# A four-layer graph network on one core: layer 0's work put in order by queues that know their buffers

## The chip, the cores and the metric

The kernel runs on one core of a Trainium2 chip. The core has five engines that each work through a queue of their own in order: TensorE (PE, matmuls), VectorE (DVE), ScalarE (ACT), GpSimd (POOL) and SyncE (SP, which here only starts transfers). They wait for one another through semaphores. The metric is the device time of one execution in microseconds (us), without the profiler. The kernel before takes 1137.64 us, the median of 3 runs (1135.74 to 1142.22). The profile is of one further execution under the hardware profiler, 1188.52 us long, with a span of 1186.5 us from the first to the last instruction.

## The reference, cut to what matters

Four graph layers on N = 4096 nodes with D = 64 features. `adj` is a dense 4096 x 4096 matrix of zeros and ones with about 4 ones in a row (probability 0.000976562).

```python
def _L0_gnn_ref(x, adj, r, w_att, b_att):            # hyperbolic attention
    c = 1.0 / r[0] ** 2
    x_t = logmap0(x, c)
    left, right = x_t @ w_att[:D, 0], x_t @ w_att[D:, 0]
    adj_att = sigmoid(left[:, None] + right[None, :] + b_att[0]) * adj
    x_local = logmap(x[:, None, :], x[None, :, :], c)
    support_t = jnp.einsum('ij,ijd->id', adj_att, x_local)
    return proj(expmap(x, support_t, c), c)
# layer 1: h_neigh = (adj @ X + X) / deg; relu([X, h_neigh] @ W + b), normalised by row
# layer 2: two hops of tanh([adj @ x, x] @ W[k])
# layer 3: weights 0.5 ** rank along each row of adj, w @ (x @ weight) + bias
h = relu(layernorm(x)); x = x + layer(h)             # around each of the four layers
```

Layer 0 needs a value for each pair of nodes that are joined. The kernel does not compute all 4096 x 4096 pairs: it finds the neighbours of each node in the matrix, gathers their rows, and computes only those.

## The kernel before: the parts that the change touches

The matrix is handled in 8 blocks `nb` of 512 columns (4 tiles of 128 nodes); two blocks make a group `g`. All layer 0 code below is written as Python generators: each `yield` is a point at which a loop at build time may switch to other work, and its number is the time which that loop assumes for the step. The order that comes out is fixed when the program is built; each engine then follows it.

Packing. A piece of a block (4 x 128 rows by 512 columns, 1 MB) is loaded, cast to fp8 for the later layers (blocks 0 to 2 stay on chip, the others are written to memory and read again after layer 0) and multiplied by powers of two on PE, so that 16 bits of the matrix become one number. `keys` holds the transposed numbers of a block in PSUM.

```python
        if part == 0:
            keys[b] = [psum.tile([P, 2, NW], F32, tag="k", bufs=2, name=f"keys{b}_{s}") for s in range(2)]
        pk = psum.tile([P, 512], F32, tag="pk", bufs=2, name=f"pk{u}")
        for v in range(4):
            at = part * 4 + v
            a = load(b, at)
            if b < EARLY:
                S.copy(a8[b][:, 4 * at : 4 * at + 4, :], a, saturate=False)
            else:
                f8 = strm.tile([P, 4, 512], FP8, tag="f8", name=f"f8_{b}_{at}")
                S.copy(f8, a, saturate=False)
                nc.scalar.dma_start(adj8[b][:, 4 * at : 4 * at + 4, :], f8.bitcast(BF16))
            bits = a.bitcast(BF16).rearrange("p j (i b) -> p j i b", b=2)
            for j in range(4):
                w = 4 * v + j
                T.matmul(
                    pk, wflat[:, w * P : (w + 1) * P], bits[:, j, :, 1], start=(w == 0), stop=(w == 15),
                )
            if v < 3:
                yield
        kt = l0w.tile([P, 512], F32, tag="kt", name=f"kt{u}")
        S.activation(kt, pk, AF.Identity, bias=num[:, part : part + 1])
        for k in range(LB):
            T.transpose(
                keys[b][k // 2][:, k % 2, part * P : part * P + P], kt[:, k * P : (k + 1) * P], sh.ident
            )
```

Lists. DVE finds for each node up to 4 neighbours (slots) and packs those that are over into a list for the block. Both parts then start gathers on GpSimd: 16 for the slots, 8 for the packed rows and their owners.

```python
    def lists(nb):
        ...
        for k in range(LB):
            kk = keys[nb][k // 2][:, k % 2, :]
            V.max(k16[:, k, :8], kk)
            V.match_replace(scr, k16[:, k, :8], kk, 0.0)
            V.max(k16[:, k, 8:], scr)
            yield 1.35
        turned[0] = nb + 1
        ...                      # neighbour numbers from the keys, into idx[nb]
        V.tensor_scalar_min(idx[nb], ji, N)
        yield 0.6
        gather_slots(nb)
        rem = tile_("rem", [LB, 48])
        cr = cand.rearrange("p k l w -> p k (l w)")
        V.tensor_tensor(rem, cr, j8[:, :, NS - 1 : NS].to_broadcast([P, LB, 48]), op=ALU.is_lt)
        V.tensor_mul(rem, rem, cr)
        ...                      # the rest into a packed list: ranks by a matmul (pb), sorted by a second (pc)
        V.tensor_scalar_min(own[nb], rw, float(N))
        yield 1.3
        gather_packed(nb)
        V.scalar_tensor_tensor(rw, ti, float(P), got[:, :, 1], op0=ALU.mult, op1=ALU.add)
        V.scalar_tensor_tensor(rw, rw, 1.0, ef, op0=ALU.add, op1=ALU.mult)
        yield 0.4
        ...
    def gather_slots(nb):
        g, q = divmod(nb, 2)
        if q == 0:
            es[g] = l0w.tile([P, 2, NE, TW], F32, tag="es", name=f"es{g}")
            hi[g] = l0w.tile([P, 2, NO, TW], F32, tag="hi", name=f"hi{g}")
        for k in range(LB):
            for s in range(NS):
                fetch(es[g][:, q, k * NS + s, :], idx[nb][:, k, s : s + 1])
```

Chunk, sums, finish. `chunk` takes the products of a gathered row with the node's own row. `sums` computes the weights, multiplies the rows by them (line 1053) and adds them up by matmuls into `v` (lines 1059 and 1065); with that the buffer `es` is free. The pool `l0w` has two buffers for each name, so `es` of group g + 2 takes the place of `es` of group g. `finish` (about 50 short operations on DVE) turns the sums of a group into its new rows of `x`.

```python
    def sums(g, q0, q1):

        part = slice(q0, q1)
        w = yield from weights(
            s_e[g][:, part, :], es[g][:, part, :, :], x2e[g][:, part, :], lfe[g][:, part, :], f"{g}_{q0}"
        )
        if q0 == 0:
            vs[g] = l0w.tile([P, 8, DQ], F32, tag="vs", name=f"vs{g}")
        for q in range(q0, q1):
            nb = 2 * g + q
            spot = l0w.tile([P, NO, 512], F32, tag="spot", name=f"spot{nb}")
            for c in range(NO):
                V.tensor_scalar(spot[:, c, :], io, rows_at[nb][:, c : c + 1], None, op0=ALU.is_equal)
                yield 0.4
            ek = es[g][:, q, :, :DQ]
            V.tensor_mul(ek, ek, bc(w[:, q - q0, :], DQ))
            yield 1.5
            bank = psum.tile([P, 512], F32, tag="v", bufs=2, name=f"v{nb}")
            pv = bank[:, : LB * DQ]
            slots = es[g][:, q, : LB * NS, :DQ].rearrange("p (k s) e -> p s k e", k=LB)
            for s in range(NS):
                T.matmul(
                    pv.rearrange("p (k e) -> p k e", k=LB), sh.ident, slots[:, s], start=(s == 0), stop=False,
                    skip_group_check=True,
                )
            for c in range(NO):
                for k in range(LB):
                    T.matmul(
                        pv[:, k * DQ : (k + 1) * DQ], spot[:, c, k * P : (k + 1) * P],
                        es[g][:, q, LB * NS + c, :DQ], start=False, stop=(c == NO - 1 and k == LB - 1),
                        skip_group_check=True,
                    )
            summed.add(nb)
            S.copy(vs[g][:, q * LB : q * LB + LB, :], pv.rearrange("p (k e) -> p k e", k=LB))
```

The order before. Lists come first whenever their keys are packed, then `chunk`, then `sums` and `finish` of a group as side work:

```python
        def can_pack():

            b, v = divmod(packed[0], 8)
            return b < NR and (v < 3 or turned[0] >= b)

        ...
        todo = [lists(nb) for nb in range(NR)]
        ...
        follow = {
            1: [sums(0, 0, 2), finish(0, 0, 8)],
            3: [sums(1, 0, 2), finish(1, 0, 8)],
            5: [sums(2, 0, 2), finish(2, 0, 8)],
            6: [sums(3, 0, 1)],
            7: [sums(3, 1, 2), finish(3, 0, 8)],
        }
        pending = []
        while listed < NR or pending or side:
            while can_pack() and arrived[packed[0]] <= now + 1.0:
                pack_one()
            job = None
            if listed < NR and packed[0] >= 8 * (listed + 1):
                job = todo[listed]
            elif pending and pending[0][1] <= now and (pending[0][0] < 4 or pending[0][0] // 2 * 2 - 3 in summed):
                job = pending[0][2]
            elif side:
                job = side[0]
        ...
```

Layer 1. `weigh` makes `y`, the weighed and normalised rows of a group in three bf16 parts, for each of four groups of 8 node tiles; `product` multiplies the matrix by it. At the first of its four steps it takes the chunks of the first three groups, then the `tail` that makes the last group, then that group's chunks:

```python
            if at == 0:
                for k in range(GR):
                    part(k, first)
                tail()
                for k in range(GR):
                    part(k, last)
                    end(k)
...
        for m in range(NQ - 1):
            weigh(m, ln_group(m, "ln1"), y3s[0], both(0), "l1", bias=b1_t)
...
        up, down = list(range(NQ)), list(reversed(range(NQ)))
        product(
            y3s[0], 3 * D + 1, "l1", up,
            lambda: weigh(NQ - 1, ln_group(NQ - 1, "ln1"), y3s[0], both(0), "l1", bias=b1_t),
            up, l1_done, lambda m: weigh(m, hs[m], y3s[1], both(1), "l2"), itself=True,
        )
```

## Time and profile before

| stretch of the span (us) | what runs | PE busy | DVE busy | POOL busy | moved, GB/s |
|---|---|---|---|---|---|
| 0 to 100 | rows of layer 0, packing, first lists | 42.15 | 58.26 | 33.51 | 268 |
| 100 to 200 | packing, lists, gathers | 42.23 | 57.72 | 65.82 | 289 |
| 200 to 300 | packing, lists | 51.68 | 67.85 | 3.46 | 277 |
| 332 to 392 | gathers of blocks 4 and 5 | 0.00 | 4.36 | 45.38 | 28 |
| 392 to 435 | sums | 13.33 | 26.07 | 0.07 | 2 |
| 435 to 495 | gathers of blocks 6 and 7 | 0.00 | 12.60 | 45.66 | 28 |
| 495 to 597 | sums and finishes | 27.24 | 59.99 | 0.00 | 1 |
| 597 to 638 | first weighings of layer 1 | 12.61 | 20.42 | 0.00 | 257 |

Over the whole span PE is busy for 699.4 us (59%), DVE for 550.2, ACT for 347.9 and POOL for 194.2. Layer 0 ends with the operation that writes `over` at 596.79 us.

How such lines are read: a row of digits is the span in 40 equal slices, and a digit is the busy share of a slice in tenths. A line of the waits names the engine and the source line that waited, after the arrow what it waited for, then the total in us, how many times, and the longest. A line of the timeline has the start and the length in us, engine, source line, operation, result and operands, and in brackets the idle time before it with what ended it. "Issue" stands for idle time which nothing in the profile explains, and "remote" for a semaphore whose writer the profile does not name.

### The profile page before, as it was taken

The page shows a single profiled execution, that of the slowest core. Times are in us where ns is not written, and L with a number is a line of the kernel's source. Part 1 is how long each engine was busy: PE and PEld are TensorE (multiplying, and loading weights), DVE is VectorE, ACT ScalarE, POOL GpSimd, SP SyncE. Part 2 cuts the span into 40 slices and gives each one's busy share as a digit, 9 for nine tenths or more (in the row PEclk, how much of TensorE's full clock was granted, in tenths as well). Part 3 has the DMA queues.
Part 4 walks back from the last instruction along what each step waited for, and adds up shares of the span by engine and source line. Part 5 has one row for each costly group of instructions (what it writes and reads, how often), then busy time and mean ns, then how long its engine had stood idle before and what let it go on. Part 6 is the DMA issues. An engine that isn't in the chain of part 4 may idle for free. (4 is left out here: it accounts for less than half of the span.)

```text
span 1186.5 us, 14354 instructions
## 1 busy us (share of the span) xinstructions
PE 699.4 (59%) x5602; PEld 527.3 (44%) x5602; DVE 550.2 (46%) x1705; ACT 347.9 (29%) x468; POOL 194.2 (16%) x208
## 2 busy tenths in 40 slices
PE   3453334456210040042226899899989779999997
PEld 1121111113110040032216899899989746565564
DVE  5746455776601622266554545422144434444443
ACT  4754344663000200113321111111112224343343
POOL 0375566000067127500000000000000000000000
PEclk9856556565565565565657999899999979999999
DMA  8788797996011001100080000000000000000000
GB/s 293 246 283 278 231 303 258 336 344 241 9 21 29 7 9 28 21 1 0 1 351 5 2 1 2 1 2 1 2 1 2 1 1 1 9 2 9 4 7 12
DMA packets 49248, 99.49 MB, mean 84 GB/s; under 512 B 6802, under 2 KB 6802, under 8 KB 48274
## 3 DMA queue, kind: packets, MB, share of 16 engines
q1 hardware_dynamic: 35232, 79.70, 19.0%
q0 software_dynamic: 6144, 6.80, 3.4%
q10 hardware_dynamic: 7794, 11.98, 2.7%
q8 instruction: 46, 0.75, 0.3%
q14 instruction: 32, 0.26, 0.1%
HBM read 85.79 MB, written 12.67 MB: 83 GB/s over the span
## 5 line engine op out<-in xcount | busy, mean ns | idle before, releaser
L1337 PEld LDWEIGHTS <-a 128*128 128x128 fp8e4 x3072 | 263.5, 98 | 12.6 <-issue 10.5
L785 PE MATMUL pk<-a,wpack 128*128 128x512 bf16 x256 | 110.4, 582 | 106.0 <-DMA a<-in_adj_t 79.5
L934 POOL DMA_INDIRECT es<-rows_d,idx x128 | 122.7, 959 | 248.5 <-PE v L1065 170.6
L1059 PE MATMUL v<-es,ident 128*128 128x260 f32 x64 | 26.3, 581 | 215.8 <-issue 208.1
L1479 DVE TENSOR_SCALAR wt<-cnt 128x512 int16<-128x512 f32 x128 | 88.5, 691 | 122.5 <-PE cnt L1472 122.5
L1480 ACT ACTIVATE wt<-cnt,low_t 128x512 int16<-128x512 f32 x128 | 87.9, 687 | 136.3 <-PE cnt L1472 136.3
L1059 PEld LDWEIGHTS v<-es,ident 128*128 128x128 f32 x64 | 17.9, 294 | 221.1 <-issue 208.5
L785 PEld LDWEIGHTS <-wpack 128*128 128x128 bf16 x256 | 32.4, 131 | 180.6 <-issue 166.5
L1459 PE MATMUL l_acc<-y_b,wt 128*128 128x192 bf16 x1024 | 107.7, 249 | 0.0
L1459 PEld LDWEIGHTS <-wt 128*128 128x128 bf16 x1024 | 90.0, 99 | 31.7 <-issue 2.4
L780 ACT CAST f<-a 128x2048 fp8e4<-128x2048 f32 x40 | 75.9, 1897 | 70.0 <-DMA a<-in_adj_t 46.4
L1337 PE MATMUL l_acc<-y_a,a 128*128 128x193 bf16 x1024 | 93.2, 250 | 3.6 <-DVE y_a L1307 3.6
L1483 PE MATMUL cnt<-a,fill 128*128 128x512 fp8e4 x248 | 81.7, 386 | 20.0 <-DVE wt L1479 20.0
L1337 PE MATMUL l2a_acc<-y_b,a 128*128 128x192 bf16 x1024 | 89.0, 249 | 2.9 <-DVE y_b L1307 2.9
L1337 PE MATMUL l2b_acc<-y_a,a 128*128 128x192 bf16 x1024 | 88.0, 247 | 3.0 <-DVE y_a L1307 3.0
L1472 PE MATMUL cnt<-a,tri 128*128 128x512 fp8e4 x256 | 77.8, 386 | 0.0
L777 ACT CAST a<-a 128x2048 fp8e4<-128x2048 f32 x24 | 45.2, 1893 | 20.7 <-DMA a<-in_adj_t 12.4
L965 DVE TENSOR_TENSOR pd<-es,tab 128x1024 f32<-128x1024 f32 x8 | 9.8, 1226 | 79.5 <-DMA es<-rows_d,idx 78.5
L1472 PEld LDWEIGHTS <-tri 128*128 128x128 bf16 x256 | 24.9, 98 | 37.3 <-issue 22.4
L793 PE MATMUL keys<-ident,kt 128*128 128x128 f32 x64 | 17.4, 425 | 39.6 <-ACT kt L791 22.7
L1483 PEld LDWEIGHTS <-fill 128*128 128x128 bf16 x248 | 24.2, 98 | 28.0 <-issue 21.3
L1065 PEld LDWEIGHTS v<-es,spot 128*128 128x128 f32 x256 | 34.6, 216 | 1.1
(336 smaller groups left out, 825.4 us busy)
## 6 DMA issues: line engine op xcount, KB each, us to landing
a<-in_adj_t SPq DMA_DIRECT2D x64, 1024.0 KB
adj<-f ACTq DMA_DIRECT2D x40, 256.0 KB
a<-adj SPq DMA_DIRECT2D x5, 2048.0 KB
es<-rows_d,idx POOLq DMA_INDIRECT x128
rows_d<-tab ACTq DMA_DIRECT2D x1, 1104.0 KB
x<-in_x SPq DMA_DIRECT2D x1, 1024.0 KB
out<-z SPq DMA_DIRECT2D x4, 256.0 KB
es<-rows_d,ovx POOLq DMA_INDIRECT x32
```

The costliest lines, as they stand in the source:

```text
L777: S.copy(a8[b][:, 4 * at : 4 * at + 4, :], a, saturate=False)
L780: S.copy(f8, a, saturate=False)
L785: T.matmul(pk, wflat[:, w * P : (w + 1) * P], bits[:, j, :, 1], start=(w == 0), stop=(w == 15),)
L934: G.indirect_dma_start(out=dst, out_offset=None, in_=rows_d, in_offset=bass.IndirectOffsetOnAxis(ap=at, axis=0))
L1059: T.matmul(pv.rearrange("p (k e) -> p k e", k=LB), sh.ident, slots[:, s], start=(s == 0), stop=False, skip_group_check=True,)
L1065: T.matmul(pv[:, k * DQ : (k + 1) * DQ], spot[:, c, k * P : (k + 1) * P], es[g][:, q, LB * NS + c, :DQ], start=False, stop=(c == NO - 1 an ...
L1337: T.matmul(acc, a8[n // 4][:, c, n % 4 * P : (n % 4 + 1) * P], y3[:, c, :cols], start=(c == first[0] and k % 2 == 0), stop=(c == last[-1] ...
L1459: T.matmul(accs[k // 2][:, k % 2, : 3 * D], wts[k // 4][:, (k % 4) * P : (k % 4 + 1) * P].bitcast(BF16), y3[:, c, : 3 * D], start=(c == NC ...
L1472: T.matmul(cnt[b], tri, masks[b], start=head_, stop=last, skip_group_check=True)
L1479: V.tensor_scalar(wts[0], cnt[0], -(128.0 - MAX_NEIGH) * UNIT, 0.0, op0=ALU.add, op1=ALU.max)
L1480: S.activation(wts[1], cnt[1], AF.Relu, bias=low_t)
L1483: T.matmul(cnt[b], fill, masks[b], start=False, stop=False, skip_group_check=True)
```

## The change

Layer 0's loop at build time is written anew. There are five queues of work: `list`, `chunk`, `sum`, `spot` and `finish`. Each piece of work knows what must be done before it, and a list stops (`HOLD`) ahead of its slot gathers until the `es` buffer that they write is free by the loop's clock. The loop counts the gathers that stand before GpSimd: with less than `BACKLOG` us of them it takes a list first, with more a chunk or a sum first. The comparison that finds a packed row's place (`spot`) is its own piece of work. The keys may take two blocks in PSUM, for which the banks of `s` and `v` fall from two to one each. In layer 1 the first product takes the chunks of `y` group by group: groups 0 and 1 are weighed, then come the matmuls of group 0, the weighing of group 2, the matmuls of group 1, the weighing of group 3, and the rest.

The diff, cut to its core (blank and unchanged lines are left out in places; "..." marks larger cuts):

```diff
@@ -47,6 +47,10 @@
 DQ = D + 1
 TW = D + 5
 NR = N // 512
+
+HOLD, FETCH = -1.0, 1000.0
+STREAM_AT, PACE_MB, PACKED = 7.0, 3.55, 5.0
+ROWS_AT, PACE_DMA, LANDED, SUMMED, BACKLOG, SLOW = 46.0, 1.27, 5.0, 6.0, 20.0, 1.1
@@ -768,7 +772,7 @@

-            keys[b] = [psum.tile([P, 2, NW], F32, tag="k", bufs=2, name=f"keys{b}_{s}") for s in range(2)]
+            keys[b] = [psum.tile([P, 2, NW], F32, tag="k", bufs=4, name=f"keys{b}_{s}") for s in range(2)]
@@ -853,7 +857,9 @@
         V.tensor_scalar(ji, ji, 2 * N - 1, None, op0=ALU.bitwise_and)
         V.tensor_scalar_min(idx[nb], ji, N)
         yield 0.6
+        yield HOLD
         gather_slots(nb)
+        yield FETCH + PACE_DMA * LB * NS
         rem = tile_("rem", [LB, 48])
         cr = cand.rearrange("p k l w -> p k (l w)")
         V.tensor_tensor(rem, cr, j8[:, :, NS - 1 : NS].to_broadcast([P, LB, 48]), op=ALU.is_lt)
...    (the one-bank change of "s" for pb and pc left out)
@@ -922,6 +928,7 @@
+        yield FETCH + PACE_DMA * 2 * NO
 ...
@@ -1033,7 +1040,14 @@
         yield 0.4
         return w
-    vs, summed = {}, set()
+    vs, spot = {}, {}
+
+    def spots(nb):
+
+        spot[nb] = l0w.tile([P, NO, 512], F32, tag="spot", name=f"spot{nb}")
+        for c in range(NO):
+            V.tensor_scalar(spot[nb][:, c, :], io, rows_at[nb][:, c : c + 1], None, op0=ALU.is_equal)
+            yield 0.48
     def sums(g, q0, q1):
@@ -1042,17 +1056,13 @@
-            vs[g] = l0w.tile([P, 8, DQ], F32, tag="vs", name=f"vs{g}")
+            vs[g] = l0w.tile([P, 8, DQ], F32, tag="vs", bufs=4, name=f"vs{g}")
-            spot = l0w.tile([P, NO, 512], F32, tag="spot", name=f"spot{nb}")
-            for c in range(NO):
-                V.tensor_scalar(spot[:, c, :], io, rows_at[nb][:, c : c + 1], None, op0=ALU.is_equal)
-                yield 0.4
-            bank = psum.tile([P, 512], F32, tag="v", bufs=2, name=f"v{nb}")
+            bank = psum.tile([P, 512], F32, tag="v", bufs=1, name=f"v{nb}")
@@ -1063,11 +1073,10 @@
-                        pv[:, k * DQ : (k + 1) * DQ], spot[:, c, k * P : (k + 1) * P],
+                        pv[:, k * DQ : (k + 1) * DQ], spot[nb][:, c, k * P : (k + 1) * P],
-            summed.add(nb)

@@ -1181,57 +1189,95 @@
             next(units[packed[0] // 4])
             packed[0] += 1
+        def arrives(m):
+            return STREAM_AT + PACE_MB * (m + 1)
         def can_pack():
             b, v = divmod(packed[0], 8)
-            return b < NR and (v < 3 or turned[0] >= b)
+            return b < NR and (v < 3 or turned[0] >= b - 1)
         row_stage(pack_one)
-...    (the loop before, whose core is shown above)
+        row_rest()
+        clock = {"now": ROWS_AT, "pool": ROWS_AT + 6.0}
+        landed, freed, done = {}, {}, set()
+        def list_ready(nb):
+            return arrives(8 * nb + 7) + PACKED if packed[0] >= 8 * nb + 8 else None
+        def list_hold(nb):
+            g = nb // 2
+            return freed.get(g - 2) if g > 1 else 0.0
+        def list_done(nb):
+            landed[nb] = clock["pool"] + LANDED
+        def sums_done(nb):
+            if nb % 2:
+                freed[nb // 2] = clock["now"] + SUMMED
+        def after(*names):
+            return lambda nb: clock["now"] if all(n in done for n in names) else None
+        class Job:
+            def __init__(self, kind, nb, gen, ready, end=None):
+                self.kind, self.nb, self.gen, self.ready, self.end = kind, nb, gen, ready, end
+                self.held = False
+        def freed_by(nb):
+            return [("sum", nb // 2 * 2 - 1)] if nb > 1 else []
+        queues = {k: [] for k in ("list", "chunk", "sum", "spot", "finish")}
+        for nb in range(NR):
+            g, q = divmod(nb, 2)
+            queues["list"].append(Job("list", nb, lists(nb), list_ready, list_done))
+            queues["chunk"].append(Job("chunk", nb, chunk(nb), landed.get))
+            queues["spot"].append(Job("spot", nb, spots(nb), after(("list", nb), *freed_by(nb))))
+            if g == NQ - 1:
+                queues["sum"].append(
+                    Job("sum", nb, sums(g, q, q + 1), after(("chunk", nb), ("spot", nb)), sums_done)
+                )
+            elif q:
+                need = [(k, n) for k in ("chunk", "spot") for n in (nb - 1, nb)]
+                queues["sum"].append(Job("sum", nb, sums(g, 0, 2), after(*need), sums_done))
+            if q:
+                queues["finish"].append(Job("finish", nb, finish(g, 0, 8), after(("sum", nb))))
+        while any(queues.values()):
+            now = clock["now"]
+            while can_pack() and arrives(packed[0]) <= now + 1.0:
                 pack_one()
+            hungry = clock["pool"] - now < BACKLOG
+            order = ["list", "chunk", "sum", "spot", "finish"] if hungry else ["chunk", "sum", "list", "spot", "finish"]
+            heads = [queues[k][0] for k in order if queues[k]]
+            times = []
+            for job in heads:
+                at = list_hold(job.nb) if job.held else job.ready(job.nb)
+                if at is not None:
+                    times.append((max(at, now), job))
+            runs = [job for at, job in times if at <= now]
+            if not runs:
+                waits = [at for at, _ in times]
                 if can_pack():
+                    waits.append(arrives(packed[0]))
+                clock["now"] = max(now + 0.1, min(waits))
                 continue
+            job = runs[0]
+            job.held = False
             try:
+                step = next(job.gen)
+                if step == HOLD:
+                    job.held = True
+                elif step >= FETCH:
+                    clock["pool"] = max(clock["pool"], now) + step - FETCH
+                else:
+                    clock["now"] = now + SLOW * step
             except StopIteration:
+                queues[job.kind].pop(0)
+                done.add((job.kind, job.nb))
+                if job.end is not None:
+                    job.end(job.nb)
         V.tensor_reduce(over, flags.rearrange("p b f -> p (b f)"), AX.X, ALU.add)
@@ -1318,7 +1364,8 @@
-    def product(y3, cols, name, made, tail, order, done, beside, itself=False):
+    def product(y3, cols, name, made, tail, order, done, beside, itself=False, behind={}):
@@ -1351,8 +1398,11 @@
                     done(m, k // 2, accs[k // 2], agg)

             if at == 0:
-                for k in range(GR):
-                    part(k, first)
+                for g in made[:-1]:
+                    for k in range(GR):
+                        part(k, range(g * GR, g * GR + GR))
+                    if g in behind:
+                        behind[g]()
                 tail()
                 for k in range(GR):
                     part(k, last)
@@ -1383,9 +1433,13 @@
         hs = {}
         V.memset(y3s[0][:, :, 3 * D : 3 * D + 1], 1.0)
-        for m in range(NQ - 1):
+        dgs = {}
+
+        def first_y(m):
             weigh(m, ln_group(m, "ln1"), y3s[0], both(0), "l1", bias=b1_t)
-        dgs = {}
+
+        first_y(0)
+        first_y(1)
         def l1_done(m, k2, acc, agg):
             if k2 == 0:
@@ -1413,9 +1467,9 @@

-            y3s[0], 3 * D + 1, "l1", up,
-            lambda: weigh(NQ - 1, ln_group(NQ - 1, "ln1"), y3s[0], both(0), "l1", bias=b1_t),
+            y3s[0], 3 * D + 1, "l1", up, lambda: None,
+            behind={0: lambda: first_y(2), 1: lambda: first_y(3)},
```

## The prediction

> **What bounds the kernel now.** I read the page's busy slices first, then the waits, then the timeline of single engines where the slices were empty. The slices (40 of them, 29.7 us each):
>
> ```profile
> PE   3453334456210040042226899899989779999997
> DVE  5746455776601622266554545422144434444443
> POOL 0375566000067127500000000000000000000000
> DMA  8788797996011001100080000000000000000000
> ```
>
> The DMA row says that the adjacency streams in until slice 9, about 300 us. From 300 to 597 us nothing streams and no engine is full; PE is busy only from slice 21 on. Those 297 us are the tail of layer 0. GpSimd (POOL) gathers neighbour rows in slices 1 to 6, not at all in 7 to 10, and again in 11 to 16. The waits of the DVE and POOL queues say why:
>
> ```profile
> POOL es L934 <- PE v L1065: 170.6, 2, 127.4
> DVE pd L965 <- DMA es<-rows_d,idx: 78.5, 3, 32.2
> ```
>
> The gathers into `es` wait for the matmuls that read the `es` of two groups before (two buffers, a group is two blocks of 512 columns): 170.6 us in two waits. The POOL timeline has both:
>
> ```profile
> 331.74 0.94 POOL L934 DMA_INDIRECT es<-rows_d,idx  x1 [127.37 <-PE v L1065]
> ...
> 434.93 0.94 POOL L934 DMA_INDIRECT es<-rows_d,idx  x1 [43.23 <-PE v L1065]
> ```
>
> And DVE, in the same stretch, starves first for keys and then for the gathers it delayed:
>
> ```profile
> 302.02 0.43 DVE L815 MAX8 k<-keys 128x8 f32<-128x256 f32 x1 [13.10 <-PE keys L793]
> ...
> 322.93 1.50 DVE L1053 TENSOR_TENSOR es<-es,w 128x1300 f32<-128x1300 f32 x1
> 353.23 1.23 DVE L965 TENSOR_TENSOR pd<-es,tab 128x1024 f32<-128x1024 f32 x1 [28.79 <-DMA es<-rows_d,idx]
> ```
>
> The product with `w` at 322.93 is the sum of block 1, though the lists of blocks 4 to 7 stand before it on DVE; only after it and its matmuls (324.49 to 331.47) may POOL gather block 4. So layer 0 runs: all lists, then two blocks of gathers (60 us), two sums, two more blocks (60 us), the rest. It is an order problem; no engine is the bound. From 597 us on the kernel is different: the chain that ended last is PE matmuls, 589 us that this change hardly touches.
>
> **Profiled and plain time.** The profiled execution took 1188.52 us, the median of the times is 1137.64: 51 us less. Layers 1 to 3 run at PE's pace, so I put the 51 us into layer 0. There DVE often waits over 1 us on nothing but its own last operation:
>
> ```profile
> 493.33 0.17 DVE L1139 TENSOR_TENSOR f_f<-f_f,f_den 128x8 f32<-128x8 f32 x1 [1.23 <-DVE f_a L1138]
> 496.13 0.17 DVE L1142 TENSOR_TENSOR f_y<-f_f,f_hs 128x8 f32<-128x8 f32 x1 [2.63 <-remote]
> ```
>
> Summed from the waits of DVE whose releaser is "DVE", "issue" or "remote": 10.8 (78 to 96 us), 14.6 (117 to 136), 8.9 (160 to 174), 5.6 (174 to 210), 21.8 (476 to 503), together 61.7, all while gathers run. I choose to read them as a cost of profiling. Layer 0 then ends at 597 - 51 = 546 us in a plain run.
>
> **What the Trainium skill says.** "Perfetto Trace Analysis", § Optimization Strategy: look at the gaps of the engine that should be full and at the semaphore that ends them; a repeated bubble can mean that there is no room for the next tile. The trace agrees: 127.4 and 43.2 us, both ended by the last reader of an `es` buffer. The same page, § DMA Instruction — SWDGE (GPSIMD): a gather's slice ends with its descriptors, not with the data. The trace agrees: the last gather of block 4 ends at 361.52, DVE reads its rows at 364.05, 2.5 us later. "SBUF — State Buffer", § SBUF: two separate sides: some DVE operations lock GpSimd out while it writes descriptors. Here it is small: the gathers average 959 ns against an undisturbed 940. "TensorE: Matmul & The Clock Gate", § What's actually happening: the array runs at half clock until it has been busy for about 3.4 us. In layer 1, 17 matmuls took 2.93 us (172 ns each) at 635 us, then 175 took 15.05 (86 ns).
>
> **The change part by part.** No operation is added or removed in layer 0; instruction counts per engine stay. What moves:
>
> 1. Lists stop before their gathers (HOLD) until the `es` buffer is free; the sums of group 0 now stand on DVE after the first half of list 3, those of group 1 before the second half of list 6. That takes away both POOL waits.
> 2. Keys get two blocks of PSUM (4 tiles for 2), so the stream no longer stops for the list of the block before; `s` and `v` fall to one bank each.
> 3. All of `finish` goes to the end but the first pieces of group 0.
> 4. Layer 1: the matmuls of y groups 0 and 1 are issued ahead of weighing groups 2 and 3.
>
> Pieces, from undisturbed stretches: a list 302.02 to 323.02, 21.0 us (11.2 to its slots); chunk 3.2; weights 412.27 to 418.14, 5.9; spots 1.6 and product 1.5 a block; finish 396.06 to 412.27, 16.2; v matmuls of two blocks 421.33 to 434.66, 13.3, of one 7.0; gathers 331.74 to 361.82, 30.1 a block (20.0 slots, 10.1 packed).
>
> Floors of the new layer 0. DVE: 50 us of rows (first list at 49.72), 8 x (21.0 + 3.2 + 1.6 + 1.5) = 218, 5 x 5.9 = 30, 4 x 16.2 = 65: 363 us. POOL: first gather 61.2, plus 8 x 30.1 = 302, plus landing, chunk, weights, product, sum and one finish, about 34: 336. Stream: 7 casts from 263.27 to 283.07 make 3.3 us a transfer, 64 of them 211 us, some 235 with disturbances. So DVE becomes the bound of layer 0.
>
> DVE does not run without gaps. Walking the new order with these pieces: list 0 done at 74 (its last part waits for block 1's packing); lists 1 and 2 at 96 and 121; list 3's slots at 141; sums of group 0 out of PE at 162, and list 3's count matmul stands behind them on PE, so DVE waits some 10 us; list 4's slots at 182, when `es` has been free since 162 and POOL has just finished block 3 (181); lists 4 and 5 at 194 and 219; list 6's slots at 234; spots, weights and products of group 1 to 246, matmuls to 260. POOL gathers block 6 from 260 to 280, its packed rows to 290, block 7 to 310 and 320. DVE: second half of list 6 to 267, list 7's first half 278, weights and product of group 2 to 285, list 7 done 296, chunk 6 at 299. The activations of block 6's weights stand on ACT behind the copy of block 5's sum (308): 5 us; weights 6 done 315, chunk 7 at 329, weights 7 and product 336. The next tanh stands behind the copy of the last sum (343), another 8 us; finish 0 done 354, then three more of 16: 402 us.
>
> Sum: layer 0 from 546 to 402, -144 us.
>
> Layer 1 before:
>
> ```profile
> 634.98 2.93 PE L1337 MATMUL l_acc<-y_a,a 128*128 128x193 bf16 x17
> 638.42 15.05 PE L1337 MATMUL l_acc<-y_a,a 128*128 128x193 bf16 x175 [0.51 <-DVE y_a L1307]
> ```
>
> PE does nothing but weighing from 597 to 635 and finishes the first eight column tiles at 666.5. A weighing takes 13.3 us; four of them end at 652. With 128 of the 256 matmuls done between weighings, 128 x 86 ns = 11 us remain after the third, of which the last 64 (6 us with the identities) after the fourth: about 659. Gain 7.5; the cold clock may eat some, I take -6.
>
> 1137.6 - 144 - 6 = 988 us.
>
> **Rivals.** (a) The DVE waits of over 1 us are real and not the profile's. Then the new order, which keeps POOL busy beside DVE almost throughout, meets them in every block: at 10 us a block, 80 us more on an engine that is now the bound; 1050 to 1070. For it: they appear only beside gathers. Against: the 51 us between profile and times need an owner. (b) The stream becomes the bound: sums put before packing on PE (13.3 us a pair) and ACT copies that wait for them hold back casts, with three stream buffers of 3.5 us each. One pair costs about 5 us, and DVE has that slack: 988 to 1000. (c) The schedule's assumed durations are off, and heads of the in-order queues block one another (PE waits for a list, DVE for PE): each 10 us more; 1000 to 1030. (d) DVE and ACT overlap better than my walk: down to the DVE floor, 363 instead of 402: 950. (e) Gathers still gate the end: POOL's 336 lies below 402, so no.
>
> **Range and chances.** (b) and (c) are more likely than (d), and (a) has perhaps one chance in seven; so 988 with 958 to 1035. Even (a) is faster by over 2% (under 1115). Slower needs a block that no part of the trace shows. Faster 0.96, same 0.02, slower 0.02.
>
> **What would show it.** Right: POOL's waits for `v` fall from 170.6 us to under 40; the DMA row ends near slice 8 or 9 of a shorter span; DVE at seven tenths or more from 50 us to the end of layer 0; `over` near 402 us plus what profiling adds; first product of layer 1 finished some 62 us after `over`, not 69.7. Wrong: POOL again waiting long for PE, DVE gaps named PE or ACT of over 10 us in a row, gaps on its own results in the plain time too, or a later stream.

## The result, and the profile after

The kernel after took 1023.8 us (median of 4 runs, 1019.2 to 1025.6), the kernel before 1136.7 us beside it (4 runs): a ratio of 0.900, 95% interval 0.895 to 0.904. Predicted were 988 us with 958 to 1035 as the range. So the direction and the mechanism held, and 36 us of the predicted gain of 150 did not come.

The busy slices of the kernel after (25.6 us each):

```profile
PE   3545556555622630017999989998996899999996
DVE  4769775769278548864455531113444345444443
POOL 0347777676067500000000000000000000000000
DMA  8699997999011100072000000000000000000000
```

The hole in the POOL row, four slices wide before, is one slice here (slice 10). DMA streams until slice 9, and PE's full stretch, layers 1 to 3, begins at slice 18. DVE has the seven tenths or more that I expected in only 9 of the 15 slices from 50 us to the end of layer 0 (2 to 16): it falls to 2 in slice 10 and to 5 and 4 in slices 13 and 14.

What POOL and DVE waited for, from the table of waits. The first line is from the waits of the whole span, the others from those of DVE between 259 and 440 us, the tail behind the last keys (line, what released it, us in total, times, longest):

```profile
POOL es L941 <- PE v L1075: 34.9, 1, 34.9
...
DVE spot L1049 <- PE v L1075: 15.9, 2, 9.2
DVE e L1018 <- ACT y L1016: 14.7, 4, 6.4
DVE f_f L1129 <- ACT f_f L1127: 10.4, 4, 9.5
DVE f_u L1096 <- ACT f_s L1114: 5.6, 1, 5.6
```

POOL's wait for `v`, 170.6 us in the profile the prediction read, is down to 34.9. What DVE waits for in the tail is neither keys nor gathers: it is the matmuls of the sums (the first of these lines) and short activations on ACT (the other three), 46.6 us in all.

The last keys and `over`, the end of layer 0, from the timelines of PE and of DVE:

```profile
259.69 1.11 PE L797 MATMUL keys<-ident,kt 128*128 128x128 f32 x4 [1.21 <-ACT kt L795]
```

```profile
439.98 0.18 DVE L1281 TENSOR_REDUCE over<-flags 128x1 f32<-128x32 f32 x1
```

From `over` to the end are 583.6 us.

### The profile page after: what moved, and what is told of

Same layout as the page of the kernel before. It is cut to its first block, busy times and chain, and to the rows that moved or that the text cites. A ratio compares the mean times of both kernels' runs of the same rounds, so it can differ in the third digit from the quotient of the medians.

```text
span 1023.6 us, 14344 instructions
## 1 busy us (share of the span) xinstructions
PE 705.4 (69%) x5602; PEld 532.8 (52%) x5602; DVE 551.8 (54%) x1705; ACT 344.2 (34%) x465; POOL 200.5 (20%) x208
## 3 DMA queue, kind: packets, MB, share of 16 engines
q1 hardware_dynamic: 35232, 79.70, 21.5%
## 4 chain that ended last, share of the span: by engine, by line
PE 49%; DVE 5%; ACT 3%; issue 1%; ACTq 0%
PE l2b_acc L1384 9%; PE l2a_acc L1384 9%; PE l_acc L1513 8%; PE l_acc L1384 8%; PE cnt L1537 7%; PE cnt L1526 5%; PE l_u L1344 1%; PE l_t L1331 1%; ACT l_h L1333 1%; DVE l_agg L1365 1%; PE l2b_u L1344 0%; PE l_u L1338 0%; DVE l_r L1351 0%; DVE ln_c L1609 0%; DVE ln_c L1615 0%
## 5 line engine op out<-in xcount | busy, mean ns | idle before, releaser
L941 POOL DMA_INDIRECT es<-rows_d,idx x128 | 128.1, 1001 | 95.3 <-issue 35.0
L1075 PEld LDWEIGHTS v<-es,spot 128*128 128x128 f32 x256 | 38.8, 238 | 1.2
L1075 PE MATMUL v<-es,spot 128*128 128x65 f32 x256 | 37.8, 318 | 0.0
L1365 DVE TENSOR_REDUCE l2a_agg<-l2a_acc 128x128 f32<-128x384 f32 x16 | 8.9, 558 | 51.4 <-PE l2a_acc L1384 51.4
```

The costliest lines, as they stand in the source:

```text
L941: G.indirect_dma_start(out=dst, out_offset=None, in_=rows_d, in_offset=bass.IndirectOffsetOnAxis(ap=at, axis=0))
L1075: T.matmul(pv[:, k * DQ : (k + 1) * DQ], spot[nb][:, c, k * P : (k + 1) * P], es[g][:, q, LB * NS + c, :DQ], start=False, stop=(c == NO - ...
```

## Experiments

Twelve runs in three groups. The groups did not meet the same chip. On chip A (first and third group) the kernel before took 1139.3 and 1138.1 us; on chip B (second group) 1182.7. Only kernels on chip A are compared with one another by their us.

**The kernel before, profiled again** (chip A; no edit).

> The kernel before, profiled a second time. My reading in the prediction: the DVE waits on its own results (61.7 us in the first profile) are a cost of profiling this kernel, so they return: a span of about 1186 us, layer 0 to its end near 597 us, plain time near 1137. Rival: that one profile was disturbed by chance; then this profile's span is within 10 us of the plain 1137 us, layer 0 ends near 547 us, and the DVE self-waits are gone, as they are in the profile of the kernel after.

Measured: a span of 1131.4 us, layer 0 ending at 541.5. The profiled execution itself took 1133.5 us, no longer than the 23 others on this chip (1134.2 to 1147.9). The waits of DVE on itself are gone: those that the trace puts down to "DVE", "issue" or "remote" make 0.6 us between 50 and 480 us; by the same count they were 53 in the first profile. The busy slices of this profile (28.3 us each), POOL's wait for the sums, and from PE's timeline the last keys of layer 0 (start, length, what it waited for):

```profile
PE   3355555461100400422268998999899689999997
DVE  5768777767015316565544554221244434444443
POOL 0367773000672177000000000000000000000000
DMA  8799999960110011000800000000000000000000
```

```profile
POOL es L934 <- PE v L1065: 149.1, 2, 105.7
```

```profile
255.86 1.12 PE L793 MATMUL keys<-ident,kt 128*128 128x128 f32 x4 [2.46 <-ACT kt L791]
```

The rival held, in this form: the first profile belongs to other conditions than the times beside it. It is not a cost of profiling. The second group points to the conditions. On chip B the kernel before takes 1182.7 us, near the first profile's 1188.5, and the kernels profiled there show the self-waits again: 61 to 98 us between 50 and 480 us, with two long waits at the spots (12.1 and 17.5 us) left out, since at the spots DVE waits for matmuls on chip A. Here is the largest group of them in one of these kernels, the version with the sums' matmuls behind the count (below):

```profile
DVE k L822 <- remote: 11.4, 6, 2.3
```

They are in the time, but on one of the two chips only. Two things follow. Taking 51 us off layer 0 led to the right start (546 against 541.5), by a wrong reason. And the second profile shows something that the first hid: on chip A the last keys of the kernel before are there at 256 us, not at 301. So 45 of the 55 us by which layer 0 is longer in the first profile lie ahead of the last keys, where the stream is. DVE is not alone in waiting there: SP, which starts the transfers, waits 58.4 us on "remote" within the first 320 us of the first profile and 4.6 in the second.

**Layer 1 alone** (chip A). The kernel before with the last two parts of the diff, layer 1's, and nothing else:

```diff
+                for g in made[:-1]:
+                    for k in range(GR):
+                        part(k, range(g * GR, g * GR + GR))
+                    if g in behind:
+                        behind[g]()
...
+            behind={0: lambda: first_y(2), 1: lambda: first_y(3)},
```

> Kernel before with the change of layer 1 alone (sums of the first y groups issued ahead of later weighings). Theory: 6 us of the gain, so about 1131 us plain, ratio 0.995; from the end of layer 0 to the end of the program 583.6 us as in the kernel after, against 589.7 before. Rival: it gains nothing by itself, because the matmuls run at half clock after the weighings' pauses: 1137, ratio 1.000, and the rest stays at 589 us.

Measured: 1135.7 us, ratio 0.996 (0.994 to 0.999). From the end of layer 0 to the end of the program: 1133.5 - 548.9 = 584.6 us, in the kernel before 1131.4 - 541.5 = 589.9. PE ahead of the fourth weighing and behind it:

```profile
586.75 7.39 PE L1337 MATMUL l_acc<-y_a,a 128*128 128x193 bf16 x64
...
599.61 6.83 PE L1337 MATMUL l_acc<-y_a,a 128*128 128x193 bf16 x72
```

64 matmuls (7.39 us) now run between the third weighing and the fourth; they are 115 ns each instead of the 86 at which PE ran 175 of them before. The gain is 5.3 us by the traces, 3.6 by the times, whose interval holds both. The theory held.

**Copies of the sums late** (chip A). In the kernel after, ACT's copy of `v` out of PSUM is issued right behind the matmuls of the sum. Here it is issued only when the bank is needed again or a `finish` begins:

```diff
+    def copies():
+        while late:
+            late.pop()()
 ...
+            copies()
             bank = psum.tile([P, 512], F32, tag="v", bufs=1, name=f"v{nb}")
 ...
-            S.copy(vs[g][:, q * LB : q * LB + LB, :], pv.rearrange("p (k e) -> p k e", k=LB))
+            late.append(
+                lambda to=vs[g][:, q * LB : q * LB + LB, :], pv=pv: S.copy(to, pv.rearrange("p (k e) -> p k e", k=LB))
+            )
 ...     (at the head of finish)
+        copies()
```

> Kernel after, with the ACT copy of each group sum out of PSUM issued only just before the bank is needed again or a finish reads it. Theory: of the 38 us that layer 0 is longer than predicted, 21 us are DVE waiting for ACT instructions that stand behind such a copy (5.9 at 345 us, 5.6 at 361, 9.5 at 383). Then layer 0 ends near 419 us and the time is about 1003 us, ratio to before 0.882. Rival: DVE only meets the matmuls of the last block a little later and waits there for the same end; then it gains under 6 us, 1018 or more.

Measured: 997.2 us, ratio to before 0.874 (0.868 to 0.880); the kernel after on the same chip (below) 1021.2. So 24 us come from moving eight instructions of 0.38 us each. How that comes about is seen best in the kernel after, in ACT's timeline, each line with its start, its length and in brackets what it waited for:

```profile
341.24 0.38 ACT L1080 COPY vs<-v 128x260 f32<-128x260 f32 x1 [6.60 <-PE v L1075]
341.63 1.28 ACT L1009 ACT_TABLE_LOAD   x1
342.93 0.22 ACT L1009 ACTIVATE w<-w 128x20 f32<-128x20 f32 x1
...
359.65 0.38 ACT L1080 COPY vs<-v 128x260 f32<-128x260 f32 x1 [13.00 <-PE v L1075]
359.93 0.63 ACT L1114 ACTIVATE f_s<-f_sup 128x512 f32<-128x512 f32 x1
...
381.54 0.38 ACT L1080 COPY vs<-v 128x260 f32<-128x260 f32 x1 [10.54 <-PE v L1075]
381.94 1.28 ACT L1127 ACT_TABLE_LOAD   x1
383.23 0.21 ACT L1127 ACTIVATE f_f<-f_a 128x8 f32<-128x8 f32 x1
```

ACT stands still for 6.6, 13.0 and 10.5 us, its queue's head waiting for PE, and the activations behind the copy (`w` and `y`, `f_s`, `f_f`) belong to other work, whose data are there. DVE in the same kernel waits for just these:

```profile
344.71 0.18 DVE L1018 TENSOR_TENSOR e<-y 128x20 f32<-128x20 f32 x1 [5.94 <-ACT y L1016]
360.59 0.69 DVE L1096 TENSOR_REDUCE f_u<-f_s 128x8 f32<-128x512 f32 x1 [5.58 <-ACT f_s L1114]
383.47 0.23 DVE L1129 SCALAR_TENSOR_TENSOR f_f<-f_f,rc_i,un_y 128x8 f32<-128x8 f32 x1 [9.53 <-ACT f_f L1127]
```

That is 21.0 us in sum. With late copies the same three instructions of DVE (the third line of code is L1137 there):

```profile
333.37 0.18 DVE L1018 TENSOR_TENSOR e<-y 128x20 f32<-128x20 f32 x1 [1.20 <-ACT y L1016]
...
343.55 0.68 DVE L1104 TENSOR_REDUCE f_u<-f_s 128x8 f32<-128x512 f32 x1
...
356.79 0.23 DVE L1137 SCALAR_TENSOR_TENSOR f_f<-f_f,rc_i,un_y 128x8 f32<-128x8 f32 x1 [0.28 <-ACT f_f L1135]
```

Two of the waits are nearly gone, and the first keeps 1.2 us, the activations themselves. DVE is busy for as long behind the last keys as in the kernel after (122.4 us against 122.5), but from the last keys to `over` it takes 413.3 - 258.9 = 154 us instead of 440.0 - 259.7 = 180. The theory held, but the 21 us are those of one profile. In the second profile of the kernel after (below) the same three waits are 5.9, 2.2 and 8.3 us, 16.4 in sum, and its tail is 16.2 us longer than with late copies. With 1.5 us left of them, 15 to 20 of the 24 us are traced to these waits. DVE's waits at the spots are 10.1 us here, 15.9 in the first profile of the kernel after and 11.0 in the second, so that difference is not shown to come from the copies.

**Spots later** (chip A). The two spots of a block are scheduled 12 us behind the sum that frees their buffers:

```diff
+        def spot_ready(nb):
+            if ("list", nb) not in done:
+                return None
+            if nb < 2:
+                return clock["now"]
+            at = freed.get(nb // 2 - 1)
+            return None if at is None else at + SPOT_LATE
 ...
-            queues["spot"].append(Job("spot", nb, spots(nb), after(("list", nb), *freed_by(nb))))
+            queues["spot"].append(Job("spot", nb, spots(nb), spot_ready))
```

> Kernel after, with the spots of a block scheduled only 12 us later than the end of the sum whose buffers they take, so that other work stands on DVE meanwhile. Theory: the two waits of DVE for matmuls at the spots of blocks 4 and 5 (9.2 and 6.7 us) are a loss on the path, DVE fills them with finish 0 and half lists, and they disappear: 16 us off, about 1008 us, ratio 0.887. Rival: DVE reaches the next wait earlier and the 16 us come back there (gathers of blocks 6 and 7 set the end): 1020 to 1026, ratio 0.90.

Measured: 1029.7 us, ratio 0.901 (0.896 to 0.907); `over` at 452.3. The waits at the spots are gone from DVE's list, the head of which is now:

```profile
DVE at L891 <- PE pb L882: 32.8, 5, 17.5
DVE f_u L1096 <- ACT f_s L1114: 18.5, 2, 10.3
...
DVE un_e L675 <- ACT un_y L673: 15.8, 4, 14.6
```

`finish 0` moved ahead, as wanted, and its activations now stood behind copies of sums: 8.3 us at 290, where ACT's copy of `v` waited for PE, and 14.6 us at 356, behind two such copies; a later `finish` 10.3 at 409. The theory failed. The waits came back, as the rival said, but not where it said, at the gathers of blocks 6 and 7 (DVE waits under 1 us for gathers here), and the time is above its range, 6 to 8 us over that of the kernel after: a gap that other work is meant to fill is worth nothing while that work needs the engine that is held up. The last keys also came 8 us later (267.8), which is not traced further.

**Less to write during the stream, kernel after** (chip B), and **with late copies** (chip A). Only the first of five fp8 blocks is written back, and layers 1 to 3 read that one for all five, so that their values are not those of the whole adjacency; 8.4 MB less are moved during the stream.

```diff
-                nc.scalar.dma_start(adj8[b][:, 4 * at : 4 * at + 4, :], f8.bitcast(BF16))
+                if b == EARLY:
+                    nc.scalar.dma_start(adj8[b][:, 4 * at : 4 * at + 4, :], f8.bitcast(BF16))
 ...
-        nc.sync.dma_start(a8[b].bitcast(BF16), adj8[b])
+        nc.sync.dma_start(a8[b].bitcast(BF16), adj8[EARLY])
```

> Kernel after, in which only the first of the five adjacency blocks that are written back as fp8 is written (layers 1 to 3 read that one block five times, so their values are not those of the reference); 8.4 MB of some 84 MB that the DMA engines move during the stream fall away. Theory: the stream is bound by the DMA engines (their share stands at 1.02 to 1.05 in most of it) and its last block is packed at 257 us instead of the 237 that I walked; with a tenth less to move it ends near 235 us, and as the tail hangs on the last keys, layer 0 ends 10 to 20 us earlier, 420 to 430 instead of 440; time 1004 to 1014. Rival: the stream waits for casts and packs (PE and ACT order), not for bytes; then its end moves by under 6 us and the time stays at 1018 to 1026.

> The late copies of sums together with four of five fp8 blocks not written back (layers 1 to 3 read one block five times, so their values are not the reference's). On a chip where the kernel with late copies takes 997 us: theory, the stream is bound by the bytes that the DMA engines move (share 1.04), 8.4 MB of 84 less end it 15 to 24 us before 259.6 and layer 0 ends 10 to 20 us before 413: time 977 to 988. Rival: the stream waits for casts, packs and lists; its end moves by under 6 us, time 990 to 999. On a chip of the slower kind the stream is uneven (slices of 142 to 340 GB/s) and I expect under 10 us of either.

On chip B: 1089.8 us, ratio 0.921 (0.917 to 0.926), last keys at 303 us. There is no run of the kernel after on that chip, so this one tells nothing of the stream; both theories stay open by it. On chip A: 984.0 us against 997.2 with late copies alone, ratio to before 0.864 (0.859 to 0.869), `over` at 398.3 instead of 413.3. The last keys of the kernel with late copies, and then of this one:

```profile
258.88 1.12 PE L797 MATMUL keys<-ident,kt 128*128 128x128 f32 x4 [1.21 <-ACT kt L795]
```

```profile
243.26 1.11 PE L798 MATMUL keys<-ident,kt 128*128 128x128 f32 x4 [0.78 <-ACT kt L796]
```

A tenth less to move brings the last keys 15.6 us earlier and the end of layer 0 by 15.0; the times differ by 13.2. The tail behind the last keys is as long as before (154 and 155 us). The theory held on chip A: what the DMA engines have to move bounds the stream. The edit also takes 32 DMA issues of 0.33 to 0.40 us from ACT's queue, but ACT is not what the stream waits for: between 50 and 260 us its casts wait 72.7 us for pieces to arrive with late copies alone, and still 63.3 us with less written. A rival stays open: SP starts a transfer only when one of the three stream buffers is free (with late copies alone it waits 163.9 us for the packing matmuls that read them), and no run varied their number.

**Keys of one block, kernel after** (chip B), and **with late copies** (chip A).

```diff
-            keys[b] = [psum.tile([P, 2, NW], F32, tag="k", bufs=4, name=f"keys{b}_{s}") for s in range(2)]
+            keys[b] = [psum.tile([P, 2, NW], F32, tag="k", bufs=2, name=f"keys{b}_{s}") for s in range(2)]
 ...
-            return b < NR and (v < 3 or turned[0] >= b - 1)
+            return b < NR and (v < 3 or turned[0] >= b)
```

> Kernel after with keys of one block again (two tiles, and packing of a block's fourth quarter transfer waits until the lists of the block before have read theirs). Theory: the second block's keys are what lets the stream run without stops, so without them the stream ends 15 to 30 us later and the time is 1040 to 1055, ratio 0.92. Rival: with sums and lists in the new order the lists follow the keys at once, and one block of keys does as well: 1020 to 1030, ratio 0.90.

> The late copies of sums, with keys of one block only. Where late copies alone take 997 us: theory, keys of two blocks are what lets the stream run on while DVE is busy with sums, so without them the stream ends 15 to 30 us later than 259.6 and the time is 1010 to 1025. Rival: lists follow their keys at once in the new order and one block does as well: 995 to 1002.

On chip B: 1094.3 us, ratio 0.926 (0.923 to 0.929); again with nothing there to compare it to. On chip A: 996.6 us, ratio 0.873 (0.868 to 0.878), against 997.2 and 0.874 with two blocks. Its last keys:

```profile
257.42 1.11 PE L797 MATMUL keys<-ident,kt 128*128 128x128 f32 x4 [1.21 <-ACT kt L795]
```

No difference in the time. With one block PE waits 5.8 us for DVE to have read the keys, and with two it never does, but the last keys come no earlier for it. The rival held: this part of the change gains nothing in the new order with late copies, on chip A.

**The assumed pace of the stream** and **the sums' matmuls behind the count** (both chip B, both with late copies), then **both together** (chip A).

```diff
-STREAM_AT, PACE_MB, PACKED = 7.0, 3.55, 5.0
+STREAM_AT, PACE_MB, PACKED = 7.0, 3.9, 5.0
```

```diff
         for q in range(q0, q1):
-            nb = 2 * g + q
             ek = es[g][:, q, :, :DQ]
             V.tensor_mul(ek, ek, bc(w[:, q - q0, :], DQ))
             yield 1.5
+        yield BEHIND
+        for q in range(q0, q1):
+            nb = 2 * g + q
             copies()
             bank = psum.tile([P, 512], F32, tag="v", bufs=1, name=f"v{nb}")
```

At `BEHIND` the loop first takes the list that stands between its slots and its count matmul on to that matmul.

> Kernel after with the late copies of sums (which took it to 997 us) and the schedule's assumed time of a transfer set to 3.9 us instead of 3.55, which is what the trace shows (64 transfers in some 250 us). The schedule then puts the weights of group 1 ahead of list 6 and its sums inside the stream. Theory: DVE has some 36 us of gaps between 100 and 250 us that such work can fill, and in the tail it is never idle for long, so what moves ahead of the last keys comes off the end: 10 to 15 us, 983 to 988, layer 0 ends near 400. Rival: the sums' matmuls on PE hold up packing and the stream ends later by as much: 993 to 1002.

> Kernel after with the late copies of sums, and the matmuls of a sum issued behind the count matmul of the list that stands beside it on DVE. The waits of DVE for that count (22.7 us in all, 9.6 at 172 us, 5.3 at 229) mostly disappear. Theory: they lie in the stretch that the stream bounds, so they cost nothing: within 5 us of 997, at most the last of them counts. Rival (what the prediction walked): DVE is the bound and each of them comes off the end: 977 to 983.

> Late copies of sums, the assumed 3.9 us a transfer, and the sums' matmuls behind the list's count matmul, together: the version that should be best. Theory, on a chip where late copies take 997: some 17 us of DVE work move ahead of the last keys, and the waits for the count (22.7 us) go; layer 0 ends at 390 to 400 instead of 413, time 974 to 986. Rival: packing is held up by as much, 992 to 1000. On a chip of the slower kind: 1060 to 1072, as its two parts alone (1075 and 1071).

On chip B: 1074.6 us (ratio 0.909, 0.904 to 0.913) and 1070.6 us (0.906, 0.902 to 0.910). Late copies alone were not run there, so neither of the two is judged. On chip A, both together: 994.2 us, ratio 0.871 (0.866 to 0.876), beside 997.2 and 0.874 (0.868 to 0.880): the intervals overlap, the two are not told apart. The last keys and DVE's waits of the version with both:

```profile
273.82 0.66 PE L797 MATMUL keys<-ident,kt 128*128 128x128 f32 x4 [0.78 <-ACT kt L795]
```

```profile
DVE spot L1056 <- PE v L1085: 21.5, 4, 8.0
...
DVE at L894 <- PE pb L884: 2.7, 4, 1.1
```

The waits for the count did go, from 22.7 to 2.7 us, and the tail fell from 154 to 409.2 - 273.8 = 135 us; but the last keys came 15 us later, and the waits at the spots doubled (10.1 to 21.5). The rival held: the matmuls of two sums run on PE from 254.9 to 268.0 us, and the stream's last packings stand behind them.

**The kernel after once more** (chip A; no edit).

> The kernel after once more, beside the other three. Runs came so far from two chips: one on which the kernel before takes some 1139 us and DVE shows no waits on its own results, and one on which it takes 1183 and DVE shows 72 to 102 us of them. Theory: those waits belong to the chip, not to the kernel or the profile, and are on the path of layer 0 there. On a chip of the first kind this run takes 1020 to 1026 us with layer 0 ending near 440; on the second kind 1085 to 1100 (ratio 0.92 to 0.93), with 70 us or more of such waits in its profile. Rival: they fall into slack, and the ratio is 0.90 on either.

Measured: 1021.2 us, ratio 0.897 (0.892 to 0.901), as expected of chip A. Its profiled run was the fastest of its four (1013.5 to 1024.4), a span of 1011.6 with `over` at 429.2 and not near 440; so one profile places the end of layer 0 to some 10 us only, and a difference of that size needs the times of several runs beside it. (Layer 0 of the run with layer 1 alone, unchanged against the kernel before, ended at 548.9 us beside 541.5.) Where the 10 us come from can be read: the matmuls of the sums, the same in both, keep PE busy for 50.3 us between 255 and 420 us in the first profile and for 41.1 in the second. One group of 32 in the first, then in the second:

```profile
352.69 6.93 PE L1075 MATMUL v<-es,spot 128*128 128x65 f32 x32
```

```profile
346.43 3.68 PE L1075 MATMUL v<-es,spot 128*128 128x65 f32 x32
```

DVE waits for these matmuls at the spots, and ACT at its copies, so the waits in the tail are longer where they are slow. What makes them slow in one execution and not in the next was not tested. What the kernel after takes on chip B was not measured, so whether the self-waits lie on its path there stays open.

**The runs on chip A side by side.** Times are medians in us, the other columns come from the one profile of each kernel; the tail is the difference of the two columns before it.

| kernel | time | last keys | end of layer 0 | tail |
|---|---|---|---|---|
| before (profiled again) | 1138.1 and 1139.3 | 255.9 | 541.5 | 285.6 |
| after | 1023.8 | 259.7 | 440.0 | 180.3 |
| after, once more | 1021.2 | 258.6 | 429.2 | 170.6 |
| after, spots later | 1029.7 | 267.8 | 452.3 | 184.5 |
| after, late copies | 997.2 | 258.9 | 413.3 | 154.4 |
| late copies, keys of one block | 996.6 | 257.4 | 414.7 | 157.3 |
| late copies, less written | 984.0 | 243.3 | 398.3 | 155.0 |
| late copies, pace 3.9, matmuls behind the count | 994.2 | 273.8 | 409.2 | 135.4 |

The change takes its gain from the tail, and the end of layer 0 is the last keys plus a tail that the order of work sets, to within the 10 us by which the two profiles of the kernel after differ. The first row of the kernel after is its first profile and the times taken beside it, from runs of chip A's kind (1136.7 us for the kernel before).

## Why the prediction was right in kind and 36 us short

**Right: the mechanism.** The gathers waited for the sums of two groups before, and the new order took that away. The waits of POOL for `v` fell from 149.1 us (chip A, before) to 34.9, under the 40 that I had set. POOL's gathers no longer stand in front of the end: DVE waits less than 1 us in all for their rows. Layer 0 went from 541.5 us to 440.0. Of the parts of the change, layer 1's brings some 5 us and the second block of keys nothing that shows; what is left of the 113 us, about 107, is the order of work. That part was not split further: holding the gathers, the early sums, the spots as pieces of their own and the new buffer counts of `vs`, `s` and `v` came together, and no run undid one of them.

**Right: layer 1.** Predicted -6; the traces show -5.3 alone and 583.6 us from `over` in the whole change, against 589.9. The first product was finished 64.6 us after `over` where I had said 62, and 70.0 before: the matmuls between the weighings took 107 to 115 ns each, not 86. I had feared the cold clock; that it is the cause is not shown.

**Right number, wrong reason: the start of the walk.** "I choose to read them as a cost of profiling": the self-waits are absent from the profiles on chip A and present in those on chip B, where the times are longer too. The profile and the times beside it were most likely taken on chips of different kinds (its 1188.5 us and its self-waits are like those of chip B, the 1137 us like those of chip A). Rival (a) is alive on chip B, where the ratio of no version was under 0.906.

**Wrong: the stream's term.** "7 casts from 263.27 to 283.07 make 3.3 us a transfer, 64 of them 211 us, some 235 with disturbances." The last keys came at 259.7 us, 64 transfers at about 4 us. The 7 casts lay in a stretch without gathers, and I allowed too little for what else moves: the DMA engines stand at 1.02 to 1.05 of their time in three of the four stretches of 50 us between 50 and 250, at 341 to 377 GB/s. This was not a changed thing at all: the kernel before, on the same chip, has its last keys at 255.9. In the walk it shows at the slots of list 6, at 251 where I had 234, 17 us. That such a delay is paid in full is what the run with less to write shows: 15.6 us earlier keys, 15.0 us earlier end.

**Wrong: part 2 of the change.** "Keys get two blocks of PSUM, so the stream no longer stops for the list of the block before". On chip A it had not stopped: in the second profile of the kernel before, PE never waits for DVE ahead of writing keys. In the first, of chip B's kind, it does for 10.3 us in three waits. The 13.10 us that the prediction shows are the other way round, DVE waiting for keys.

**Wrong: the tail.** From list 6's slots on I walked 402 - 234 = 168 us, it took 440 - 251 = 189. I had two of the three waits behind copies of sums ("5 us" and "another 8 us"; they measured 5.9 and 9.5) and missed the third (5.6), the wait of group 1's weights for an activation that stood behind the stream's last cast (6.4), and those at the spots (9.2 and 6.7), which I had costed at 1.6 us a block without asking who still read their two buffers. These four make 28 us, against 21 that the tail is longer in all (with the stream's 17 that is 440 - 402 = 38). That is the first profile. In the second, list 6's slots are again at 251, the tail from there is 178 us, and the same four are 18.6 us against 10. The difference goes back to the matmuls of the sums, for which the walk had 13.3 us a pair and 7.0 for one: those of group 1 took 18.9 us in the first profile and 14.0 in the second, those of block 6 10.5 and 7.1. As the four waits are more than the excess in both profiles, the walk had 7 to 8 us too much elsewhere. The walk thus took the waits behind copies as given; the run with late copies shows that they were a choice of the change: undoing it is worth 24 us.

**The rivals.** Of (b) the first half came true, the stream ends later than walked, but little of it by its reason: with a pair of sums ahead of packing the last keys came at 259.7, and in the kernel before, with the sum of one block ahead of its last packing, at 255.9. (c) came true, heads of queues blocked one another, and the time lies in the range that I gave it; I had treated the two as alternatives. (d) is the opposite of what came: behind the last keys DVE is busy 122.5 of 180 us. (e) fell as expected. One of my signs of being wrong came, the later stream, and one in part: a gap of DVE that is named PE, 10.5 us before a list's count, which the walk had at "some 10".

A version better than both kernels exists: with late copies 997.2 us, 24 less than the kernel after on the same chip.

## What to carry to other kernels

When work is reordered over queues that run in order, look at each engine's queue, not only the bound one: a cheap instruction that waits for another engine, like a copy out of PSUM issued as soon as it can be written down, holds up everything behind it, and belongs as late as its buffer allows. Measure the pace of a stream in the stretch where all its neighbours run too, and ask what the stream is bound by before crediting a buffer to it. And before a difference between a profile and its times is explained, or one of 10 us between two profiles, profile the kernel a second time.

## What the runs showed of the hardware

On two chips the same kernel before took 1138 and 1183 us. On the second, DVE pauses on nothing that the trace names but its own last result (or on "issue" or "remote"): 61 to 98 us in sum, 1.1 to 1.2 us at a time on average and 4.5 at most, and only in layer 0, where gathers and stream run. Layers 1 to 3 take as long on either: from `over` to the end 1059.4 - 477.2 = 582.2 us in a kernel on chip B, 583.3 with late copies on chip A. The stream is slower there as well: the last keys came at 288 to 324 us in the four kernels profiled on chip B, and at 243 to 274 in those on chip A. What causes the pauses and the slower stream stays open; no run here varied it, and only one chip of each kind was met for certain.

The same group of 32 matmuls of a sum took 6.93 us in one execution of the kernel after and 3.68 in another, 1.9 times as long, and such differences go with an end of layer 0 that moved by some 10 us.

Beside a busier DVE the gathers became little slower: those into the slots of `es` average 1001 ns in the kernel after, 959 before. What the Trainium skill says of DVE operations that lock GpSimd out ("SBUF — State Buffer", § SBUF: two separate sides) is thus a matter of 42 ns apiece here at the most, if it is the cause, on an engine that no longer sets the end. The median gather takes 944 ns in both kernels; a few are longer, up to 2.26 us against 1.69.
